# Inverse roots of four values per partition by a power on GpSimd

## The chip, the cores and the metric

The kernel runs on one core of a Trainium2 chip. The metric is the device time in microseconds from launch to the end of the program, the median of several executions. The engines are named as the profile names them: PE is TensorE (PEld its weight loads), DVE is VectorE, ACT is ScalarE, POOL is GpSimd and SP is SyncE, which issues most of the DMAs. Each engine works through its own queue in order, and waits on semaphores for the others.

## The reference

A residual stream x of four sequences of 512 rows and 128 features goes through twelve sublayers in four groups. Each group is half a feed-forward layer, a full attention layer, and the same feed-forward layer again, each on the normalized stream:

```python
def _layernorm(x, axis=-1, eps=1e-05):
    m = jnp.mean(x, axis=axis, keepdims=True)
    v = jnp.var(x, axis=axis, keepdims=True)
    return (x - m) / jnp.sqrt(v + eps)
...
    x = x + 0.5 * _L0_ffn_ref(_layernorm(x, axis=-1), ...)
    x = x + _L0_attn_ref(_layernorm(x, axis=-1), ...)
    x = x + 0.5 * _L0_ffn_ref(_layernorm(x, axis=-1), ...)
    x = x + 0.5 * _L1_ffn_ref(_layernorm(x, axis=-1), ...)
...
    x = x + 0.5 * _L3_ffn_ref(_layernorm(x, axis=-1), ...)
```

Group 0 has a feed-forward layer that selects neurons and a local attention with relative positions. Group 1's feed-forward layer is a transformer block with causal attention, two more layer norms (`var + LN_EPS` under an inverse root, LN_EPS 1e-5) and eight experts; its attention is linear, on queries and keys divided by their lengths. Group 2 has a feed-forward layer that sends each row to one of eight experts, and a block-local attention. Group 3's feed-forward layer is two transformer layers with windowed attention on unit-length queries and keys and a layer norm of its own; its attention is dense.

Inverse square roots stand in all the layer norms and in the unit lengths.

## The kernel before

The stream x stays in SBUF as 16 tiles of 128 rows by 128 features, four tiles to a sequence b, and y holds the normalized stream. A layer norm of a sequence is `statistics` (line 207): for each of its four tiles a BATCH_NORM_STATS and a BATCH_NORM_AGGREGATE on DVE, which give mean and variance in `ln_mv`, and then one `inverse_root` over the four variances of a partition, a 128x4 operand, into `ln_r`. Then `scaled` (line 220) writes the four tiles of y on DVE, one instruction each (L225), and `turn` (line 249) transposes them on PE (`pt_y`) and copies them on ACT to `yT` (L254), from which the sublayer's products read.

`inverse_root` (line 188) is an approximation: L195 adds or clips by a constant, L196 makes a first guess from the bits of the number, and two rounds refine it, each of three instructions on DVE (L198, L200, L201) or four on POOL (L198, L203, L204, L205). So it is eight small instructions on DVE or ten on POOL. All the calls, by width n:

- n = 4, on DVE: 52 calls of `statistics`. 48 are for the stream, four sequences at each of the twelve sublayers; four are group 1's own layer norms of the last sequence.
- n = 4, on POOL: 12 calls of `statistics` for group 1's own layer norms of the other three sequences (`l1_experts`, line 992). Their result goes to `scaled_by_act` (line 236), two small POOL instructions and four on ACT.
- n = 4 on POOL in 14 units of group 3's feed-forward layer (`variance`, line 1786), n = 4 on DVE in one unit, and n = 2 on DVE twice at the very end. There the variances come from a product with ones (`pvar`), DVE copies them to `rs` (L1793), and the result spreads over a diagonal `dg` on DVE (L1801, in `spread`) which a product (`pb`) carries to all partitions.
- n = 16 on POOL, 64 calls (`project`, line 1667), and n = 128 on DVE, four calls (`scale` of the linear attention, line 1142).

The order of the work has two sources. Products on PE, most of ACT and some of DVE are kept in the order of the program (`mm_in_order`, `keep_in_program_order`); which sequence's normalization runs beside which step is written into the program by chains of deferred parts (`chain`, `tick`, `leave_normed`). The remaining instructions of DVE and POOL are put in order at compile time by a planner which runs the program on its own estimates of durations; on the chip the queues are then worked in that fixed order.

POOL's other work matters where the change puts something into its queue:

- Group 1's causal attention: an affine select after each pair of exponentials (L835), which waits for ACT.
- Group 2's feed-forward layer ends with 16 indirect DMAs on POOL, one per tile (L1371), that gather the experts' rows into y. They are all issued in `l2_slots` ahead of the updates of x (L1379), which come sequence by sequence and are each followed by `leave_normed` with `statistics`.
- Group 3's feed-forward layer: sums and scalings of 128x1024 and 128x512 (L1668, L1669, L1731), and the n = 16 inverse roots.

Of the kernel before, what the change touches and what calls it, by code (L numbers as in the profile page):

```python
# [23 lines left out]
F32, I32 = mybir.dt.float32, mybir.dt.int32  # L24
AF = mybir.ActivationFunctionType
ALU = mybir.AluOpType
AX = mybir.AxisListType

P = 128
B, S, D, H, HD = 4, 512, 128, 16, 8  # L30
NT = B * S // P
TB = S // P
# [71 lines left out]
def tile_macaron(ctx, tc, x_in, const_in, vec_in, w0_in, ws_in, ws3_in, w2f_in, w3_in, out):  # L104
    nc = tc.nc
    pool = lambda name, **kw: tc.tile_pool(name=name, bufs=1, **kw)

    keep = ctx.enter_context(pool("keep"))
# [41 lines left out]
    make_identity(nc, ident)  # L150
    onesm = keep.tile([P, P], F32, name="onesm")
    nc.gpsimd.memset(onesm, 1.0 / D)
    ones = keep.tile([P, P], F32, name="ones")
    nc.gpsimd.memset(ones, 1.0)

# [32 lines left out]
    def inverse_root(sb, dst, src, name, op, c, eng=None):  # L188


        n = src.shape[-1]
        v = sb.tile([P, 3, n], F32, tag=name, name=name, bufs=2)
        eng = eng or nc.vector
        xx, yy, t = (v[:, i, :] for i in range(3))
        eng.tensor_scalar(xx, src, c, None, op)  # L195
        eng.tensor_scalar(yy.bitcast(I32), xx.bitcast(I32), -0.5, float(0x5F1FFFF9), ALU.mult, ALU.add)  # L196
        for to, a, b in ((yy, -0.703952253, 1.681913895), (dst, -0.50000016, 1.50000048)):
            eng.tensor_mul(t, yy, yy)  # L198
            if eng is nc.vector:
                eng.scalar_tensor_tensor(t, t, a, xx, ALU.mult, ALU.mult)  # L200
                eng.scalar_tensor_tensor(to, t, b, yy, ALU.add, ALU.mult)  # L201
            else:
                eng.tensor_mul(t, t, xx)  # L203
                eng.tensor_scalar(t, t, a, b, ALU.mult, ALU.add)  # L204
                eng.tensor_mul(to, t, yy)  # L205

    def statistics(src, b, eng=None, pinned=False):

        st = keep.tile([P, TB, 6], F32, tag="ln_st", name="ln_st", bufs=2)
        mv = keep.tile([P, TB, 2], F32, tag="ln_mv", name="ln_mv", bufs=3)  # L210
        r = keep.tile([P, TB], F32, tag="ln_r", name="ln_r", bufs=3)
        for t in range(TB):
            first = nc.vector.bn_stats(st[:, t, :], src[:, b * TB + t, :])
            if pinned and t == 0:
                tc.keep_in_program_order(first)
            nc.vector.bn_aggr(mv[:, t, :], st[:, t, :])
        inverse_root(keep, r, mv[:, :, 1], "ir4", ALU.add, 1e-5, eng)
        return mv, r
# [897 lines left out]
    def l1_attn(vms):  # L1116
        with pool("l1a") as sb, banks("l1aps", d=2, m=3, o=1):
# [19 lines left out]
            def scale(b):  # L1137

                qkv, vm = seqs[b]["qkv"], vms[b % 2]
                rn = sb.tile([P, TB * 32], F32, tag="rn", name="rn")  # L1140
                nc.vector.tensor_reduce(rn, seqs[b].pop("sq").rearrange("p t (h d) -> p (t h) d", d=HD), AX.X, ALU.add)
                inverse_root(sb, rn, rn, "ir128", ALU.max, 1e-24)
                beta = sb.tile([P, TB, H], F32, tag="beta", name="beta")
                nc.vector.tensor_add(beta, qkv[:, :, 384:400], rows(VEC(vec, "1a_bb"), TB))
                nc.scalar.activation(beta, beta, AF.Sigmoid)
                qk = qkv[:, :, 0:256].rearrange("p t (h d) -> p t h d", d=HD)
                r4 = rn.rearrange("p (t h) -> p t h", t=TB)[:, :, :, None].to_broadcast([P, TB, 32, HD])
                nc.vector.tensor_mul(qk, qk, r4)
                for t in range(TB):
                    a = vm[:, t, 0, 0:1]  # L1150
                    to = bass.AP(a.tensor, a.offset, [list(a.ap[0]), [32, 4], [D + HD, 4], [1, HD]])
                    nc.vector.tensor_mul(
                        to, qkv[:, t, 256:384].rearrange("p (g j d) -> p g j d", g=4, j=4),
                        beta[:, t, :].rearrange("p (g j) -> p g j", g=4)[:, :, :, None].to_broadcast([P, 4, 4, HD]),
                    )
# [437 lines left out]
    def l3_ffn(w3, tag, first, rb):  # L1593
        with pool(tag) as sb, banks(tag + "ps", d=3, m=2):
# [48 lines left out]
            def project(step):  # L1643
# [21 lines left out]
                rn = sb.tile([P, 16], F32, tag="rn", name="rn", bufs=6)  # L1665
                nc.vector.tensor_reduce(rn, sq, AX.X, ALU.add)
                inverse_root(sb, rn, rn, "ir16", ALU.max, 1e-24, nc.gpsimd)
                nc.gpsimd.tensor_add(t1, t1, t2)  # L1668
                nc.gpsimd.tensor_mul(t1[:, 8:16, :], t1[:, 8:16, :], bcast(rn[:, 8:16], 64))  # L1669
# [411 lines left out]
```

## Time and profile before

| | |
|---|---|
| median of three runs | 2732.9 us (2726.75 to 2735.28) |
| profiled execution | 2729.0 us |
| its span, first to last instruction | 2726.9 us |
| mean granted TensorE clock | 0.88 |
| PE busy | 2191.1 us (80%) |
| DVE busy | 1808.4 us (66%) |
| ACT busy | 1267.1 us (46%) |
| POOL busy | 905.4 us (33%) |

The program is a long row of stages with different limits, so a share of the whole span says little of one place. The views of the trace used below are the groups by tile (durations as least, median and largest, with who waited for them), the table of waits (engine and line, what it waited for, total us, times, longest), and the timeline (start, duration, engine, line, operation, what it writes and reads, and in brackets the idle time of the engine before it and what ended it).

### The profile page before, as it was taken

To read this page: it belongs to the slowest core of one execution; us is meant where nothing else is said; L and a number is where in the kernel's file an instruction comes from. 1 tells how busy PE (TensorE), PEld (TensorE's weight loads), DVE (VectorE), ACT (ScalarE), POOL (GpSimd) and SP (SyncE) were. 2 spreads that over 40 slices of the span, in tenths; PEclk is the share of its full clock that TensorE was granted. 3 is DMA by queue.
4 is the path that set the end of the run, shared out by engine and by line. 5 is a ranking of instruction groups with operands and counts; after the bars stand their busy time and mean duration, and the time that the engine had idled before them with its cause. 6 is when DMAs were issued, how large, how long until landed. Compare 5 with 4: busy or idle time off the path is not lost. (4 is left out here: it accounts for less than half of the span.)

```text
span 2726.9 us, 49905 instructions
## 1 busy us (share of the span) xinstructions
PE 2191.1 (80%) x18572; PEld 1226.1 (45%) x18572; DVE 1808.4 (66%) x5013; ACT 1267.1 (46%) x3067; POOL 905.4 (33%) x1678
## 2 busy tenths in 40 slices
PE   4277539988779999948666868898899999789888
PEld 2145214443334444438456745555433333455555
DVE  4746487777566777563664487777567775877774
ACT  3054314444333544314332356776525554667764
POOL 1012012233122222213321377766300000877761
PEclk8578769998789999868886889999879999899998
DMA  3053010000000000008104611000000000100000
GB/s 143 0 158 93 0 63 1 1 1 1 1 1 1 1 2 5 5 21 300 37 10 160 200 27 24 21 21 20 1 0 1 1 1 7 28 20 21 22 21 12
DMA packets 33930, 99.31 MB, mean 36 GB/s; under 512 B 6200, under 2 KB 12344, under 8 KB 33176
## 3 DMA queue, kind: packets, MB, share of 16 engines
q1 hardware_dynamic: 30760, 88.03, 10.0%
q0 software_dynamic: 2496, 5.12, 0.8%
q8 instruction: 146, 2.39, 0.4%
q10 hardware_dynamic: 432, 2.98, 0.3%
q14 instruction: 96, 0.79, 0.1%
HBM read 66.88 MB, written 14.55 MB: 30 GB/s over the span
## 5 line engine op out<-in xcount | busy, mean ns | idle before, releaser
L832 ACT ACTIVATE PT<-pk_at 128x512 f32<-128x512 f32 (+3 forms) x768 | 335.2, 488 | 405.4 <-PE pq_at L171 259.3
L171 PE MATMUL pk_at<-qx,km 32*128 32x512 f32 (+3 forms) x1536 | 398.8, 554 | 4.6 <-ACT PT L832 2.7
L804 DVE CUSTOM_DVE_ANT_0 s<-pq_at,cst 128x384 f32<-128x384 f32 (+3 forms) x512 | 249.9, 488 | 96.0 <-PE pq_at L171 42.5
L171 PE MATMUL pq_at<-km,qT 32*128 32x128 f32 (+3 forms) x1024 | 274.0, 500 | 16.0 <-DVE nm L804 12.0
L1607 ACT ACTIVATE s<-s,nm,rn 128x128 f32<-128x128 f32 x512 | 245.5, 482 | 0.9 <-DVE nm L1719 0.7
L835 POOL TENSOR_SCALAR_AFFINE_SELECT PT<-PT 128x256 f32<-128x256 f32 x256 | 104.5, 410 | 388.7 <-ACT PT L832 387.7
L171 PEld LDWEIGHTS pk_at<-qx,km 32*128 32x128 f32 x1536 | 146.7, 190 | 153.3 <-issue 92.9
L171 PE MATMUL po_at<-PT,vh 128*32 128x128 f32 (+3 forms) x2432 | 205.6, 394 | 8.5 <-POOL PT L835 8.4
L806 DVE TENSOR_REDUCE nm<-pq_at 128x1 f32<-128x512 f32 x256 | 165.6, 685 | 57.6 <-PE pq_at L171 57.2
L1668 POOL TENSOR_TENSOR t<-t,t 128x1024 f32<-128x1024 f32 x64 | 151.8, 2372 | 123.4 <-DVE t L1664 123.1
L171 PE MATMUL pq_at<-km,t 32*128 32x512 f32 x512 | 175.0, 670 | 1.6 <-DVE nm L806 1.2
L168 PE MATMUL pt_y<-ident,y 128*128 128x128 f32 x224 | 52.3, 362 | 132.2 <-DVE y L225 104.9
L171 PE MATMUL p_qk<-w,hT 128*128 128x512 f32 x256 | 141.9, 682 | 8.8 <-DVE t L1664 6.0
L254 ACT COPY yT<-pt_y 128x512 f32<-128x512 f32 x56 | 32.8, 585 | 239.1 <-PE pt_y L168 238.6
L168 PE MATMUL pt<-ident,s 128*128 128x128 f32 x640 | 93.0, 293 | 62.0 <-POOL s L1731 38.9
L1731 POOL TENSOR_TENSOR s<-s,sm 128x1024 f32<-128x1024 f32 x64 | 121.6, 1901 | 49.1 <-DVE sm L1730 41.0
L171 PEld LDWEIGHTS po_at<-PT,vh 128*32 128x32 f32 x2432 | 53.8, 109 | 173.3 <-issue 119.8
L171 PEld LDWEIGHTS pq_at<-km,qT 32*128 32x128 f32 x1024 | 110.2, 189 | 46.6 <-DVE nm L804 26.8
L1607 ACT ACTIVATE sq<-p_qk 128x1024 f32<-128x1024 f32 x64 | 65.6, 1026 | 118.4 <-PE p_qk L171 65.8
L168 PEld LDWEIGHTS pt<-ident,s 128*128 128x128 f32 x640 | 78.2, 150 | 93.7 <-POOL s L1731 48.1
L1661 DVE TENSOR_TENSOR t<-p_qk,w 128x1024 f32<-128x1024 f32 x64 | 78.2, 1223 | 55.7 <-ACT sq L1607 55.6
L1349 DVE SCALAR_TENSOR_TENSOR hT<-pa,w,sg 128x128 f32<-128x128 f32 x184 | 51.9, 345 | 85.4 <-ACT sg L1348 63.6
(435 smaller groups left out, 5167.6 us busy)
## 6 DMA issues: line engine op xcount, KB each, us to landing
w<-in_w2f_dram SPq DMA_DIRECT2D x46, 836.0 KB, 6.2
vb<-v SPq DMA_DIRECT2D x112, 128.0 KB, 2.2
skew<-qe SPq DMA_DIRECT2D x16, 512.0 KB, 3.0
rel<-skew SPq DMA_DIRECT2D x64, 128.0 KB, 3.5
w<-in_w_dram SPq DMA_DIRECT2D x1, 4147.0 KB, 12.5
w<-in_w_dram SPq DMA_DIRECT2D x1, 3200.0 KB
od<-o SPq DMA_DIRECT2D x46, 64.0 KB, 5.1
yd<-y SPq DMA_DIRECT2D x8, 256.0 KB, 2.3
```

Of the source, the lines that this page charges most:

```text
L168: return nc.tensor.transpose(dst, src, ident[: src.shape[0], : src.shape[0]])
L171: tc.keep_in_program_order(nc.tensor.matmul(dst, lhsT=lhsT, rhs=rhs, start=start, stop=stop))
L254: by_order(nc.scalar.copy(yT[:, b, :], pt))
L804: nc.vector.tensor_tensor_reduce(s[:, :nk], pq[:, :nk], causal[:, S - nk :], 1.0, -BIG, ALU.add, ALU.max, to)
L806: nc.vector.tensor_reduce(to, pq, AX.X, ALU.max)
L832: by_order(nc.scalar.activation(PT[:, i, q0:], pk[:, q0:], AF.Exp, scale=SC8))
L835: nc.gpsimd.affine_select(d, d, pattern=[[0, 2], [1, P]], base=0, channel_multiplier=-1, compare_op=ALU.is_ge, fill=0.0)
L1349: nc.vector.scalar_tensor_tensor(hT[s][:, c, :], pa[:, ts(c, P)], b1[:, c : c + 1], sg, ALU.add, ALU.mult)
L1607: tc.keep_in_program_order(nc.scalar.activation(*args, **kw))
L1661: nc.vector.tensor_mul(by_head(t1), by_head(p3), over(tab[:, 0]))
L1668: nc.gpsimd.tensor_add(t1, t1, t2)
L1731: nc.gpsimd.tensor_mul(s, s, bcast(sm, P))
```

## The change

Where n is at most 4, `inverse_root` now keeps its first instruction (add or clip) on the engine of the call, and POOL then raises the result to the power of a tile that holds -0.5, straight into the destination. The tile `minus_half`, 128x4, is set once at the start by a memset on POOL. The 16- and 128-wide calls are as before.

```diff
     onesm = keep.tile([P, P], F32, name="onesm")
     nc.gpsimd.memset(onesm, 1.0 / D)
+    minus_half = keep.tile([P, TB], F32, name="minus_half")
+    nc.gpsimd.memset(minus_half, -0.5)
...
         n = src.shape[-1]
+        if n <= TB:
+            v = sb.tile([P, n], F32, tag=name, name=name, bufs=2)
+            (eng or nc.vector).tensor_scalar(v, src, c, None, op)
+            nc.gpsimd.tensor_tensor(dst, v, minus_half[:, :n], ALU.pow)
+            return
         v = sb.tile([P, 3, n], F32, tag=name, name=name, bufs=2)
         eng = eng or nc.vector
```

## The prediction

> **What bounds the kernel now.** I read the page first: PE is busy 80% of the span and no engine is full, so stages and waits decide. The chain of waits can be followed only from 1812 us to the end; before that I go by the waits themselves. Then I asked for the tile `ir`, in which the inverse roots are made, for the table of waits, and for the timeline at three kinds of call.
>
> The tile `ir` (durations in ns, least/median/largest), then who waited for it:
>
> ```profile
> L198 POOL TENSOR_TENSOR ir<-ir x180: 198/215/218, 487.9 to 2682.6; 128x16 f32<-128x16 f32 x128, 128x4 f32<-128x4 f32 x52
> ...
> L198 DVE TENSOR_TENSOR ir<-ir x118: 127/161/2341, 11.7 to 2710.6; 128x4 f32<-128x4 f32 x106, 128x128 f32<-128x128 f32 x8, 128x2 f32<-128x2 f32 x4
> ...
> L205 POOL TENSOR_TENSOR rs<-ir x14: 198/199/202, 1666.2 to 2683.4; 128x4 f32<-128x4 f32 x14
> ...
>   DVE dg L1801: 47.1, 14
> ```
>
> A small two-input instruction on POOL takes 0.20 us, on DVE 0.16. DVE sits 47.1 us behind POOL's roots in group 3. The table of waits has the other end:
>
> ```profile
> POOL PT L835 <- ACT PT L832: 387.7, 215, 24.4
> ...
> PE pt_y L168 <- DVE y L225: 104.9, 21, 15.1
> ...
> POOL ln_m L240 <- DVE ln_r L201: 33.8, 2, 26.1
> ```
>
> 21 times PE stands still until a normalized tile comes: there the latency of the root counts in full. One such place, in the timeline:
>
> ```profile
> 1428.57 0.17 DVE L195 TENSOR_SCALAR ir<-ln_mv 128x4 f32<-128x4 f32 x1
> ...
> 1429.96 0.16 DVE L201 SCALAR_TENSOR_TENSOR ln_r<-ir 128x4 f32<-128x4 f32 x1
> 1430.16 1.12 DVE L225 TENSOR_SCALAR y<-x,ln_mv,ln_r 128x128 f32<-128x128 f32 x4
> ...
> 1430.65 1.15 PE L168 MATMUL pt_y<-ident,y 128*128 128x128 f32 x4 [2.61 <-DVE y L225]
> ```
>
> From the start of L195 to the start of L225 it is 1.59 us. The second kind, a unit of group 3:
>
> ```profile
> 2541.55 1.91 POOL L1731 TENSOR_TENSOR s<-s,sm 128x1024 f32<-128x1024 f32 x1
> ...
> 2543.54 0.23 POOL L195 TENSOR_SCALAR ir<-rs 128x4 f32<-128x4 f32 x1
> ...
> 2544.68 1.02 ACT L1607 ACTIVATE sq<-p_qk 128x1024 f32<-128x1024 f32 x1 [1.55 <-PE p_qk L171]
> ...
> 2546.11 0.20 POOL L205 TENSOR_TENSOR rs<-ir 128x4 f32<-128x4 f32 x1
> ...
> 2546.34 0.69 DVE L1801 SCALAR_TENSOR_TENSOR dg<-ident,rs 128x512 f32<-128x512 f32 x1 [3.32 <-POOL rs L205]
> ...
> 2546.95 1.22 DVE L1661 TENSOR_TENSOR t<-p_qk,w 128x1024 f32<-128x1024 f32 x1
> ```
>
> Ten POOL instructions take 2.77 us; L1661 could have started at 2545.71, when `sq` was done, and starts 1.3 us later. The third kind, after the gathers of group 2:
>
> ```profile
> 1307.58 0.94 POOL L1371 DMA_INDIRECT y<-od,at  x1 [20.22 <-DMA od<-o]
> ...
> 1326.34 0.94 POOL L1371 DMA_INDIRECT y<-od,at  x1 [0.31 <-issue]
> ...
> 1315.92 0.17 DVE L195 TENSOR_SCALAR ir<-ln_mv 128x4 f32<-128x4 f32 x1
> ...
> 1319.62 1.11 DVE L225 TENSOR_SCALAR y<-x,ln_mv,ln_r 128x128 f32<-128x128 f32 x4
> ...
> 1320.11 1.15 PE L168 MATMUL pt_y<-ident,y 128*128 128x128 f32 x4 [15.13 <-DVE y L225]
> ```
>
> Here the first sequence's root is made on DVE while POOL issues gathers one every 1.25 us, until 1327.28. The other feed-forward layer of group 2 ends the same way: gathers from 1544.00 to 1563.67, L225 at 1557.86, PE idle 8.81 until 1558.34.
>
> **The change part by part.** It removes seven DVE instructions at 55 calls (52 in `statistics`, three in group 3), 385 in all, some 71 us of DVE's busy time, and nine POOL instructions at 26 calls, 234 x 0.20 = 46 us. It adds 81 powers on POOL, a hop from DVE to POOL and back at 55 calls, and one memset of about 0.1 us at the start, which lies beside the first loads and costs nothing unless POOL holds the first call up.
>
> *The power, T.* No row shows one. It is no cheaper than the 128x4 product, 0.20. The far end is the ten-instruction root on POOL, 2.77, though nothing in the trace excludes more. The first end would mean that a power costs what a product does, so I build it up: 128x1024 takes 2.37 us (L1668) and 128x4 0.20, so one pass costs 2.1 ns a column. The exponent is a tensor, so the instruction must serve any exponent; I assume 100 to 150 elementary steps a column. That is 0.2 + 4 x (0.21 to 0.32) = 1.05 to 1.5. I take 1.3, and keep 0.2 and 2.77 for the range.
>
> [...]
>
> *The 55 calls on DVE.* After: L195 0.17, hop to POOL 0.14 (L1664 ends 2549.36, POOL's L1668 starts 2549.50), T, hop back 0.03 (2546.31 to 2546.34), so 0.34 + T against 1.59: even at T = 1.25. I count 23 places that are not hidden: 14 of the 21 PE waits (without the two at the gathers, one in group 3, and second tiles of the same sequence), the two `ln_m` waits, and seven in group 3 that the chain goes through. At T = 1.3: 23 x 0.05 = +1 us. The other calls lie beside PE work; their cover gone, each costs the same 0.05.
>
> *The 14 units of group 3.* The root on POOL goes from 2.77 to 0.28 + 1.3 = 1.58, 1.19 less. What is late next is `sq`: L1661 starts after it by 1.73, 1.32, 0, 0.16, 1.32, 0.89, 1.79, 0, 0.81, 1.32, 0, 0 us in the twelve full units, which caps the gain. With 1.19 as the limit that is 7.8, and 2 x 1.19 for the two last units of the layers, 10.2. POOL's sums and DVE's masks recur in the same loop, so I take 70%: -7.
>
> The 12 POOL calls of group 1 get 1.4 us shorter each. ACT's PE-bound exponentials cover them (6.3 us of waits on `ir` in all): 0.
>
> *The gathers.* All 16 stand in the program ahead of the updates, so I expect the first sequence's power behind the last of them. Its L225 then starts at 1327.31 + 1.3 + 0.03 instead of 1319.62, 9.0 late; in the second place at 1563.71 + 1.3 + 0.03 instead of 1557.86, 7.2 late. PE, which waits for exactly this, moves with it. Recovered: the second sequence's statistics, 2.9 us of DVE work after L225 now, can be done in the wait. +16.2 - 3 = +13. If the planner puts the power among the gathers, it is 0 (rival 3).
>
> *POOL's queue elsewhere.* Behind the power on POOL, and behind L225 on DVE, stand others: in group 1's attention affine selects that wait on average 1.8 us (387.7/215) for ACT, and on DVE the row maxima (L804), for whose banks PE waits. Five calls lie there: 5 x 1.8 = 9 if nothing covers it, 0 if the planner leaves room. PE works on the maxima five steps ahead (LEAD, line 718), so I take +4. Late in group 2 and in the first layers of group 3 DVE's small instructions are now held beside POOL's big ones (L198, 2341 ns at most against 161): seven fewer to be held, but L225 held in their place. 0, with 4 us either way.
>
> Sum: +1 - 7 + 13 + 4 = +11, so 2740 against the profiled execution's 2729.0 (its span 2726.9 and 2.1 around it). That execution stands 3.9 below the median of the three runs, 2732.9; on the median's footing it is 2744.
>
> **The rivals.** *1, faster: a short power.* At T = 0.5 the DVE calls give 23 x -0.75 = -17, the units -9 (all of the slack, 13.3 x 0.7), gathers +12, queues +3: -11, median 2722. It decides below T of about 0.6. For it: POOL's 16-wide rows cost hardly more than the 4-wide (215 against 198), so four columns may share their steps. Against it: no POOL row does more than one pass. Chance 0.25.
>
> *2, a long power.* At T = 1.8, columns one after the other: +13 - 4.5 + 14 + 5 = +27, median 2760. At 2.77: 23 x 1.52 = +35, units +3, gathers +16, queues +7 = +61, median 2794. At 5, each lane for itself: +86 +25 +21 +10 = +142, median 2875. Chance 0.28, of which 0.12 for near 1.8 and 0.08 for above 3.9.
>
> [...]
>
> *3, the gathers don't matter,* because the planner sets the power between them: T = 1.3 gives +1 - 7 + 4 = -2, no change, median 2731. For it: in the second place DVE takes the next sequence's update (L1379) between L195 and L196 of the first, so the planner thinks gathers quick. Chance 0.10.
>
> **How the numbers follow.** My forecast, T between 0.9 and 1.6 with the gathers in front, has 0.37, and 2744 is its time. Its own range is 2735 to 2753. For 8 in 10 I go down into rival 1 to T = 0.25 (23 x -1.0, -9, +11, 0 = -21, 2712) and up to T = 3.9 (some +100, 2835); about 0.1 stays out at each end. A measurement here can tell some 0.3%, 8.2 us. Faster by more (below 2724.7): three quarters of rival 1 and small parts of the forecast and rival 3, 0.25. Slower by more (above 2741.1): rival 2 and 0.6 of the forecast, 0.53 with a little of rival 3. Within: 0.22.
>
> **What would show it.** In the changed profile: a POOL row of 81 powers (128x4, two of 128x2) at about 1.3 us; the wait of `dg` on POOL's `rs` down from 3.3 to about 2.1 us each; L225 after the gathers at some 20 us after the first gather where it is 12 now, with PE's wait there up from 15.1 to 24; DVE some 70 us less busy. A power under 0.6 or over 1.8 makes the forecast wrong, and so does a power issued between two gathers, or another order on DVE that moves a whole stage.

## The result and the profile after

The changed kernel was first measured at 2720.1 us (median of seven executions, 2715.65 to 2726.1) beside 2735.28 for the kernel before (seven, 2726.75 to 2743.29): a ratio of 0.9951, 95% interval 0.9934 to 0.9967, so 13.4 us faster (18.1 to 9.0). The prediction was 2744, slower. Two later measurements of the same two kernels gave 1.0009 (0.9993 to 1.0025, no difference) and 0.9962 (0.995 to 0.9975, faster). So the question is also why one change has two results; the experiments answer most of it.

The profiled execution took 2719.6 us, its span 2716.7 (before: 2729.0 and 2726.9). The first part of the page after, busy time of each engine:

```profile
PE 2180.3 (80%) x18572; PEld 1222.5 (45%) x18572; DVE 1753.8 (65%) x4628; ACT 1267.3 (47%) x3067; POOL 943.6 (35%) x1526
```

DVE has 385 instructions fewer, as counted, and is 54.6 us less busy (1808.4 before), where the prediction had 71; POOL is 38.2 us more busy. The kernel has seven lines more above `statistics`, so the old L225 is now L232, L1801 is L1808, and the power is L197.

The groups of the tile `minus_half`, which every power reads (least/median/largest in ns), and who waited for them:

```profile
L197 POOL TENSOR_TENSOR ln_r<-ir,minus_half x64: 1002/1018/1546, 11.4 to 2307.1; 128x4 f32<-128x4 f32 x64
L197 POOL TENSOR_TENSOR rs<-ir,minus_half x17: 697/1037/1251, 1674.5 to 2700.2; 128x4 f32<-128x4 f32 x15, 128x2 f32<-128x2 f32 x2
...
  DVE y L232: 61.0, 43
  DVE dg L1808: 29.1, 16
```

Here are the 81 powers. T is 1.02 us at 128x4 and 0.70 at 128x2, so about 0.16 a column and 0.38 besides. DVE now waits 61.0 us for layer-norm roots, a wait that did not exist, and 29.1 us over 16 places for those of group 3 (47.1 over 14 before). The table of waits has the same from PE's side:

```profile
POOL ln_r L197 <- DVE ir L196: 388.5, 36, 107.3
POOL PT L842 <- ACT PT L839: 384.3, 218, 23.6
...
PE pt_y L170 <- DVE y L232: 74.3, 21, 12.9
...
PE pt_y L170 <- issue: 39.6, 2, 23.9
```

In the first row POOL stands at a power until DVE has done its first instruction; the 33.8 us that it waited at L240 for DVE's roots are gone into it. PE's two long waits behind the gathers (15.1 and 8.8 us before) are the 39.6 us of the last row, filed under "issue", for which the profile shows no releaser; without them 74.3 us are left where 104.9 less 23.9, so 81.0, stood before. The three kinds of call in the timeline, first the open place that stood at 1428.57:

```profile
1433.13 0.17 DVE L196 TENSOR_SCALAR ir<-ln_mv 128x4 f32<-128x4 f32 x1
1433.38 1.01 POOL L197 TENSOR_TENSOR ln_r<-ir,minus_half 128x4 f32<-128x4 f32 x1 [6.45 <-DVE ir L196]
1434.43 1.12 DVE L232 TENSOR_SCALAR y<-x,ln_mv,ln_r 128x128 f32<-128x128 f32 x4 [1.12 <-POOL ln_r L197]
```

From L196 to L232 it is 1.30 us, 1.59 before. A unit of group 3, with what comes behind its root:

```profile
2536.68 1.04 POOL L197 TENSOR_TENSOR rs<-ir,minus_half 128x4 f32<-128x4 f32 x1
...
2537.51 1.03 ACT L1614 ACTIVATE sq<-p_qk 128x1024 f32<-128x1024 f32 x1 [1.55 <-PE p_qk L173]
...
2537.75 0.69 DVE L1808 SCALAR_TENSOR_TENSOR dg<-ident,rs 128x512 f32<-128x512 f32 x1 [1.91 <-POOL rs L197]
...
2538.57 1.23 DVE L1668 TENSOR_TENSOR t<-p_qk,w 128x1024 f32<-128x1024 f32 x1
```

DVE waits 1.91 us for the root, 3.32 before, and L1668 now starts 0.03 after `sq` is done (2538.54): the slack is used up, as the prediction had it. And behind the first gathers:

```profile
1326.17 0.94 POOL L1378 DMA_INDIRECT y<-od,at  x1 [0.30 <-issue]
1327.14 2.05 POOL L197 TENSOR_TENSOR ln_r<-ir,minus_half 128x4 f32<-128x4 f32 x2
```
```profile
1328.72 1.15 PE L170 MATMUL pt_y<-ident,y 128*128 128x128 f32 x4 [23.86 <-issue]
```

The power stands behind the last gather, and PE waits 23.86 us for the tile where it waited 15.13; it starts 8.6 us later than before (1320.11). All of this is what the prediction described. Yet the total was the other way.

### The profile page after: what moved, and what is told of

It reads as the page before. It is cut to its first block, busy times and chain, and to the rows that moved or that the text cites. A ratio compares the mean times of both kernels' runs of the same rounds, so it can differ in the third digit from the quotient of the medians.

```text
span 2716.7 us, 49358 instructions
## 1 busy us (share of the span) xinstructions
PE 2180.3 (80%) x18572; PEld 1222.5 (45%) x18572; DVE 1753.8 (65%) x4628; ACT 1267.3 (47%) x3067; POOL 943.6 (35%) x1526
## 3 DMA queue, kind: packets, MB, share of 16 engines
q1 hardware_dynamic: 30760, 88.03, 10.2%
## 4 chain that ended last, share of the span: by engine, by line
PE 55%; DVE 23%; POOL 8%; ACT 8%; issue 5%; DMA 2%; POOLq 0%; DVEq 0%; SPq 0%; ACTq 0%
PE pk_at L173 10%; PE po_at L173 6%; PE pa L173 4%; PE pq_at L173 4%; PE pag L173 3%; PE po L173 3%; ACT s L1614 2%; PE pe L173 2%; PE p_qk L173 2%; DVE t L1671 2%; PE pg L173 2%; DVE t L1668 2%; PE pz L173 2%; POOL ln_r L197 2%; PE pt L170 2%
## 5 line engine op out<-in xcount | busy, mean ns | idle before, releaser
L842 POOL TENSOR_SCALAR_AFFINE_SELECT PT<-PT 128x256 f32<-128x256 f32 x256 | 104.8, 411 | 384.4 <-ACT PT L839 384.3
L197 POOL TENSOR_TENSOR ln_r<-ir,minus_half 128x4 f32<-128x4 f32 x64 | 65.9, 1032 | 389.8 <-DVE ir L196 388.5
L170 PE MATMUL pt_y<-ident,y 128*128 128x128 f32 x224 | 52.5, 360 | 138.5 <-DVE y L232 74.3
L173 PE MATMUL p_qk<-w,hT 128*128 128x512 f32 x256 | 136.6, 660 | 13.1 <-DVE t L1671 10.3
L1668 DVE TENSOR_TENSOR t<-p_qk,w 128x1024 f32<-128x1024 f32 x64 | 78.2, 1223 | 58.3 <-ACT sq L1614 57.5
```

The costliest lines, as they stand in the source:

```text
L170: return nc.tensor.transpose(dst, src, ident[: src.shape[0], : src.shape[0]])
L173: tc.keep_in_program_order(nc.tensor.matmul(dst, lhsT=lhsT, rhs=rhs, start=start, stop=stop))
L197: nc.gpsimd.tensor_tensor(dst, v, minus_half[:, :n], ALU.pow)
L842: nc.gpsimd.affine_select(d, d, pattern=[[0, 2], [1, P]], base=0, channel_multiplier=-1, compare_op=ALU.is_ge, fill=0.0)
L1668: nc.vector.tensor_mul(by_head(t1), by_head(p3), over(tab[:, 0]))
```

## The experiments

Names: the units are the roots of group 3 (14 on POOL; the runs that change them change the three short roots of DVE with them), "the gathers' calls" the eight `statistics` behind the two sets of gathers, "POOL's calls" the 12 of group 1. Differences in us are the ratio less one, times the median of the kernel before in the same measurement, with the 95% interval in brackets. Two traces are lined up by PE's instructions, which come in the same order in both: the difference of their starts shows where one kernel gains or loses.

### First measurement: parts of the change, and twice its length

**Steps behind the gathers.** The eight calls keep the approximation steps, all others have the power:

```diff
-        if n <= TB:
+        if n <= TB and not steps:
...
-            leave_normed(b, spare, gap, True)
+            leave_normed(b, spare, gap, True, steps=True)
```

> The power everywhere but in the eight calls right after the two sets of gathers, which go back to the eight steps on DVE. Theory A (each place counts for itself): the changed kernel starts the stage after the gathers 8.6 and 6.9 us late, and of the first 4.8 is caught up later, so this one is some 11 us faster than the changed kernel, 21 to 27 below the kernel before; PE's first product after the gathers comes about 12.5 us after the first gather again. Rival B (the delay is absorbed by what follows, or replaced by another wait): within 4 us of the changed kernel, 10 to 16 below the kernel before.

Measured 0.9972 (0.9956 to 0.9989): 7.6 us below [12.0, 3.0]. Neither case: taking the delay away gained nothing over the changed kernel.

**The units alone.** The power only in `spread`'s roots:

```diff
-        if n <= TB:
+        if power:
...
-                inverse_root(rb, rs[:, :n], rs[:, :n], f"ir{n}", ALU.add, 1e-5, eng)
+                inverse_root(rb, rs[:, :n], rs[:, :n], f"ir{n}", ALU.add, 1e-5, eng, True)
```

> The power in group 3's own layer norm alone (17 calls: 14 units on POOL, one on DVE, two halves at the end), the old steps everywhere else. Theory A: the units give 12 us (the sum of the changes of PE's time from unit to unit in the changed profile) and the ends of the two layers 2 to 6: 13 to 18 us below the kernel before. The forecast's own term was 7. Rival B (group 3's gain in the changed profile comes from another order of DVE and POOL or from the clock, not from the shorter root): under 5.

Measured 0.998 (0.9957 to 1.0002): 5.5 below [11.7 below, 0.5 above], with executions from 2715.7 to 2734.9. Not settled by this run.

**DVE's 52 calls alone,** the gathers' among them:

```diff
+        inverse_root(keep, r, mv[:, :, 1], ..., ALU.add, 1e-5, eng, eng is None or eng is nc.vector)
```

> The power in the 52 calls of the layer norms on DVE alone, POOL's calls and group 3's units as before. Theory A: the gathers cost 11 net, some 21 other open places give 0.2 us each and what DVE is spared gives a little more: 0 to 8 us above the kernel before. Rival B (these calls gain more than the gathers cost, by the shorter DVE queue): 3 or more below it.

Measured 1.0018 (1.0003 to 1.0032): 4.9 above [0.8, 8.7]. It fits the first case, but the trace gave a reason to doubt the reading, below.

**Twice the power.** A power with exponent 1 ahead of each:

```diff
-            nc.gpsimd.tensor_tensor(dst, v, minus_half[:, :n], ALU.pow)
+            nc.gpsimd.tensor_tensor(v2, v, ones[:, :n], ALU.pow)
+            nc.gpsimd.tensor_tensor(dst, v2, minus_half[:, :n], ALU.pow)
```

> Every root is made by two powers, one with exponent 1 and then the one with -0.5, so each is 1.0 to 1.1 us longer, all else as in the changed kernel. Theory A with all the open places of the forecast (23 calls on DVE, 14 units, two gathers): 30 to 40 us above the changed kernel, 15 to 28 above the kernel before. Rival B (most places have slack): less than 12 above the changed kernel, still not slower than the kernel before.

Measured 1.0196 (1.0161 to 1.0232): 53.5 above before [44.0, 63.4]. The first of the two powers took 1.04 us at the median (1001 to 1546 ns) and the second 1.01, so an exponent of 1 costs what -0.5 costs. That is more than either case allowed. Against the changed kernel, some 10 below before where it was measured under the same conditions (fourth measurement), it is some 64 us for about 1.04 more in 81 places, as if some 60 of the 81 were open at that length. A part may be the clock: its mean was 0.8728 against 0.8817 for before beside it, and among the 25 executions of before 0.001 of clock goes with 1.8 us, which would make some 16 of the 64. The prediction had counted 23 open calls, 14 units and the gathers. Cover that is enough for a root of 1.6 us seems not to be enough for one of 2.3.

**What the traces showed.** In the first two of these kernels nothing behind the gathers was changed, and still PE stood 4 to 7 us later there than in the trace of before. DVE's instructions of 0.16 us came one every 1.40 us in the second place (1563.43, 1564.84, 1566.23, 1567.63, 1569.03 in the first kernel), each released late by the one ahead of it. In the trace of before they follow each other by 0.20. The kernels with the tile `minus_half` have all later tiles further on in SBUF (by 32 bytes of a partition, as the next expectation reckons; no view shows it), y among them, into which the gathers write; so the next measurement tried the place of y.

### Second measurement: the place of y

**The tile alone,** no power:

```diff
     nc.gpsimd.memset(onesm, 1.0 / D)
+    minus_half = keep.tile([P, TB], F32, name="minus_half")
+    nc.gpsimd.memset(minus_half, -0.5)
```

> The kernel before with the tile minus_half and its memset and nothing else: no power anywhere. The tile takes 32 bytes of a partition, so y and all tiles behind it begin 32 bytes later. In the traces of the two kernels that keep the approximation steps after the gathers, DVE's instructions there are released only every 1.40 us (1563.43, 1564.84, 1566.23, 1567.63, 1569.03, each 0.16 long), and PE gets its next product 4.1 us late after the first set of gathers and 6.3 us late after the second. Theory P (the place of y does it): the same stalls here, both places together some 10 us, so 6 to 12 us above the kernel before, without any change of the roots. Theory C (chance of one profiled execution, or something that the powers do): no such spacing here, and the time within 3 us of before.

Measured 1.0016 (1.0 to 1.0032): 4.4 above [0.0, 8.7]. Theory P falls: the trace has no late releases behind the gathers. The median alone would not have told it, for the identical program later came out 3.0 above itself.

**Steps behind the gathers, with a tile of 64 bytes:**

```diff
-    minus_half = keep.tile([P, TB], F32, name="minus_half")
+    minus_half = keep.tile([P, 16], F32, name="minus_half")
```

> As in the run that keeps the approximation steps in the eight calls after the gathers and uses the power everywhere else, but minus_half is 128x16, 64 bytes of a partition, so y lies 64 bytes later than before instead of 32. Theory P: the stalls behind the gathers go away, some 10 us, so 15 to 21 us below before, where that run was 7.2 below; it is then 3 to 8 us below the changed kernel of the same job. Theory C: as that run, 4 to 11 below before, not below the changed kernel. Either way no call in it waits behind the gathers, so if it comes out level with the changed kernel, the 8.6 and 7.0 us by which PE starts later behind the gathers there are not what the total shows.

Measured 2711.09, 0.9968 (0.9956 to 0.9981): 8.7 below [12.0, 5.2]. That is theory C's size, but the kernel is 13.7 below the changed kernel of the same measurement (2724.82, next), which C excluded. No late releases in the trace.

**The changed kernel again:**

> The changed kernel itself, for a second trace and for a comparison within this job. Both theories: ratio to before near 0.995, 10 to 18 us below. In the trace L232 behind the gathers is about 20.8 us after the first gather again, and the stretch of the half clock near 681 to 698 us of the kernel before may or may not come back: if it does, its 7 us were never the roots'.

Measured 2724.82 beside 2720.22, 1.0009 (0.9993 to 1.0025): 2.4 above [1.9 below, 6.8 above]. Not the first result: the kernel before is 15 us faster than beside the first result (2735.28), the changed one is 5 slower (2720.1).

**The changed kernel with the tile of 64 bytes:**

> The changed kernel with minus_half 128x16, so that y lies as it does in the run with the steps kept and the wide tile. Behind the gathers DVE has nothing to do here but to wait for the power, so slow releases cost little. Theory P: within 4 us of the changed kernel, a little faster if anything (PE's first eight products there took 6.78 us instead of 5.94). Theory C: the same within 3 us.

Measured 2725.14, 1.0018 (1.0004 to 1.0031). The width of the tile does nothing (2724.82 with 16 bytes). And against the kernel that differs only in the gathers' calls, 2711.09, these calls cost 14.0 us here.

So in this measurement nobody's releases were late, whatever the place of y, and in the one before all four kernels had them late or were waiting for the power at that time. That leaves the kernel before itself as the one that changes.

### Third measurement: the kernel before again, and two parts

**The kernel before:**

> The kernel before itself, for a second trace of it. Theory S (on some chips DVE's releases are slow while the gathers write, whatever the kernel; the first four experiments ran on one such chip and the next four did not): either the trace has the releases spaced by 1.2 to 1.4 us in the second set of gathers and PE's 4.1 us wait in the first, and then the median is near 2731; or it has neither, and then it is near 2720. Theory L (the kernels with the power cause it): never slow here, and the median may lie anywhere from 2720 to 2733. The half clock at 681 to 698 us: no forecast; if it is absent the stretch 668 to 712 takes about 37 us instead of 44.

Measured 2723.34 beside 2720.55, 1.0011 (0.9997 to 1.0024): the same program differs from itself by 3.0 [0.8 below, 6.5 above], which is what these comparisons are good for. The releases are prompt.

**The power in the gathers' calls alone,** against the kernel with the steps there:

```diff
-        if n <= TB and not steps:
+        if n <= TB and steps:
```

> The power only in the eight calls behind the two sets of gathers, everything else as before (minus_half 128x16). The first trace gave PE a start 8.6 and 7.0 us later there, with 4.8 made up in the first place. Theory G (that delay stays in the total): 10 to 16 above before if the releases there are prompt in the kernel before; with slow releases, which cost before some 10 us that this kernel hides behind its own wait, 0 to 6 above. Theory H (made up later): within 4 of before on a chip with prompt releases.

Measured 1.0064 (1.0047 to 1.0082): 17.4 above [12.8, 22.3]. Theory G, a little above its range: the delay stays in the total. PE's first wait there is 23.87 us. Lined up with the second trace of before, PE loses 8.8 us at the first gathers, wins 4.5 back and loses 7.0 at the second, 11 in all; the two kernels that differ in these calls alone (2711.09 and 2725.14) are 13.5 apart there. So not all of the 17.4 is seen at the gathers.

**The units alone,** tile of 64 bytes:

> The power only in group 3's 14 units, minus_half 128x16. The root there goes from 2.77 us to some 1.3 us (0.23 for the first instruction, 1.02 for the power), 1.5 less, capped by the slack before sq (10.3 us in the rows of twelve units) and two tails of 1.5. Theory U (the slack sets the gain): 8 to 14 below before. Rival (POOL's sums and DVE's masks take it back): 0 to 6 below.

Measured 0.9955 (0.9939 to 0.997): 12.2 below [16.6, 8.2]. Theory U: the slack sets the gain.

**The 16-wide roots as one power too,** on the kernel with the steps behind the gathers:

```diff
-        if n <= TB and not steps:
+        if n <= 16 and not steps:
```

> The 64 roots of sixteen values on POOL as one power as well, on top of the kernel that keeps the steps behind the gathers (minus_half 128x16). Rows: 128x4 in 1.02 us, 128x2 in 0.70, so 0.16 a column and 0.38 fixed, and 128x16 would take 2.9; the ten instructions from the start of L195 to the end of L205 take 3.0 (1570.78 to 1573.76). Theory W (cost grows by the column): rows of 2.8 to 3.0 us plus 0.3 for the first instruction, time within 4 us of 2711's place, that is 5 to 13 below before. Rival V (columns share their steps beyond some width): rows of 1.2 to 2 us, and 4 to 12 us faster than that.

Measured 0.997 (0.9958 to 0.9982): 8.2 below [11.4, 4.9]; that kernel without it was 8.7 below. Theory W. Its row, by the tile `minus_half`:

```profile
L197 POOL TENSOR_TENSOR rn<-ir,minus_half x64: 2928/2929/3147, 1570.7 to 2633.2; 128x16 f32<-128x16 f32 x64
```

2.93 us for 16 columns: 0.70, 1.02 and 2.93 lie on one line, 0.16 a column. Columns share nothing but the 0.38. The ten instructions take 3.0 us for 16 columns and 2.77 for four, so the gain is gone at 16.

### Fourth measurement: both kernels where releases are late

**The kernel before, and the changed kernel:**

> The kernel before once more, for what it does on a chip with slow releases. If the job's chip is one: the releases behind the gathers spaced by 1.2 to 1.4 us, PE some 4 and 6 us later there than in the two traces of it so far, and a median near 2731. If not: near 2720 to 2723, and the releases prompt.

> The changed kernel on the same chip. With slow releases in the kernel before: 10 to 16 below it. With prompt ones: 0 to 7 above it, as in the second measurement (2.4 above, interval 1.9 below to 6.8 above).

Before: 2731.82 beside 2732.32, 0.9999 (0.9985 to 1.0013). Changed: 0.9962 (0.995 to 0.9975), 10.4 below [13.7, 6.8]. This time the kernel before has the late releases itself. Its third trace, DVE behind the second gathers:

```profile
1563.39 0.16 DVE L196 TENSOR_SCALAR ir<-ir 128x4 int32<-128x4 int32 x1
1564.95 0.16 DVE L198 TENSOR_TENSOR ir<-ir 128x4 f32<-128x4 f32 x1 [1.40 <-issue]
1567.05 0.17 DVE L200 SCALAR_TENSOR_TENSOR ir<-ir 128x4 f32<-128x4 f32 x1 [1.94 <-remote]
1567.79 0.16 DVE L201 SCALAR_TENSOR_TENSOR ir<-ir 128x4 f32<-128x4 f32 x1 [0.57 <-DVE ir L200]
1569.18 0.16 DVE L198 TENSOR_TENSOR ir<-ir 128x4 f32<-128x4 f32 x1 [1.23 <-DVE ir L201]
```

and its second trace, the same instructions of the same program:

```profile
1551.00 0.16 DVE L196 TENSOR_SCALAR ir<-ir 128x4 int32<-128x4 int32 x1
1551.19 0.16 DVE L198 TENSOR_TENSOR ir<-ir 128x4 f32<-128x4 f32 x1
1551.39 0.16 DVE L200 SCALAR_TENSOR_TENSOR ir<-ir 128x4 f32<-128x4 f32 x1
1551.59 0.16 DVE L201 SCALAR_TENSOR_TENSOR ir<-ir 128x4 f32<-128x4 f32 x1
1551.78 0.16 DVE L198 TENSOR_TENSOR ir<-ir 128x4 f32<-128x4 f32 x1
```

Behind the first gathers it is PE that stands, in the third trace, with a releaser that the profile cannot name:

```profile
1322.70 3.78 PE L171 MATMUL p<-yT,ws 128*128 128x512 f32 x4 [0.73 <-issue]
1330.51 3.78 PE L171 MATMUL p<-yT,ws 128*128 128x512 f32 x4 [4.02 <-remote]
```

where the second trace has the eight products in one go:

```profile
1314.69 5.88 PE L171 MATMUL p<-yT,ws 128*128 128x512 f32 x8 [0.73 <-ACT yT L254]
```

Lined up, the third trace falls behind the second by some 5 us at the first gathers and some 6.5 at the second, 11 to 12 in all. The medians beside them differ by as much (2732.3 and 2720.6), but the two spans by 25.3: the third trace loses another 6.6 near 690, where its clock stood at 0.50, and the rest in small pieces. And the mean clock of before was lower too in this measurement, 0.8810 against 0.8838 in the third, so that the medians alone could not tell the releases from the clock; the rows above do. The changed kernel has DVE and PE waiting for the power during just these microseconds. Its trace here, lined up with that of the second measurement, loses nothing at either set of gathers (0.0 us). It pays its 8.6 and 7.0 us there in either case, and nothing on top.

**POOL's calls alone:**

```diff
+        inverse_root(keep, r, mv[:, :, 1], ..., ALU.add, 1e-5, eng, eng is not None and eng is not nc.vector)
```

> The power only in the 12 calls of group 1 that are made on POOL, everything else as before (minus_half 128x16). Each gets about 1.5 us shorter. Theory N (ACT's exponentials cover them, as the prediction had it): within 3 us of before. Rival (POOL's queue reaches the affine selects earlier): 3 to 8 below.

Measured 0.9964 (0.9952 to 0.9976): 9.8 below [13.1, 6.6], more than the rival said. In the second trace of before POOL works two of these roots at once, and what is behind them are the affine selects (L835):

```profile
1090.42 0.41 POOL L195 TENSOR_SCALAR ir<-ln_mv 128x4 f32<-128x4 f32 x2 [1.05 <-DVE ln_mv L216]
...
1094.70 0.41 POOL L241 TENSOR_SCALAR ln_m<-ln_m 128x4 f32<-128x4 f32 x2
1095.07 0.41 POOL L835 TENSOR_SCALAR_AFFINE_SELECT PT<-PT 128x256 f32<-128x256 f32 x1
```
```profile
1098.66 3.18 ACT L244 ACTIVATE y<-y,ln_m,ln_r 128x128 f32<-128x128 f32 x8
```

With the power (here L842 is the select, L251 the scaling):

```profile
1086.74 0.41 POOL L196 TENSOR_SCALAR ir<-ln_mv 128x4 f32<-128x4 f32 x2 [1.05 <-DVE ln_mv L223]
1087.12 2.02 POOL L197 TENSOR_TENSOR ln_r<-ir,minus_half 128x4 f32<-128x4 f32 x2
...
1089.93 0.77 POOL L842 TENSOR_SCALAR_AFFINE_SELECT PT<-PT 128x256 f32<-128x256 f32 x2
```
```profile
1092.54 3.18 ACT L251 ACTIVATE y<-y,ln_m,ln_r 128x128 f32<-128x128 f32 x8
```

The select comes 3.19 us after the root's start instead of 4.65, ACT's scaling 5.80 instead of 8.24. PE's instructions lined up, the third trace of before against this one, move forward by 0.5 to 2.5 us at six of these places (0.5 at 580, 1.5 at 650, 1.6 at 720, 1.1 at 950, 2.5 at 1100, 0.9 at 1170). Near 970 they fall 2.7 back, where this trace has the clock at 0.50 (962.4 to 969.2) and that one has not.

**DVE's 44 calls away from the gathers:**

```diff
+        inverse_root(keep, r, mv[:, :, 1], ..., ALU.add, 1e-5, eng, (eng is None or eng is nc.vector) and not steps)
```

> The power in the 44 calls on DVE that don't stand behind the gathers, everything else as before (minus_half 128x16). From the start of the first instruction to the start of the scaling such a call went from 1.59 to 1.30 us in the trace of the changed kernel. Theory D (the 23 open places gain 0.29 each): 4 to 9 below before. Rival Q (the powers in POOL's queue, and another order on DVE, cost as much): 2 below to 6 above. The difference of the two kernels measured so far (the units alone 12.2 below; units, POOL's calls and these 44 together 8.7 below) speaks for Q.

Measured 1.0022 (1.0011 to 1.0033): 6.0 above [3.0, 9.0]. Rival Q: the calls got shorter and the kernel slower. The traces show where: PE's instructions that stand at 540 to 1240 us in the second trace of before, nearly all of group 1, take 699.8 us there, 706.8 in the third trace and 712.5 here. Elsewhere this kernel is no slower than the third trace. PE is busy 591.6 us of that stretch, against 582.8 and 587.7, at the same instructions and a lower granted clock, so a good part of the loss is longer products and not waiting alone (columns: window, length, busy time of PE, PEld, DVE, ACT and POOL, granted clock, DMA share, GB/s; second trace, third trace, this kernel):

```profile
540.18:1240.02 699.84, 582.82 (x4330) 290.20 (x4323) 470.25 (x1805) 265.21 (x647) 183.11 (x401) 0.89 0.03 10
542.08:1248.91 706.83, 587.72 (x4329) 292.38 (x4322) 470.25 (x1805) 265.13 (x647) 183.00 (x401) 0.88 0.03 10
539.76:1252.24 712.48, 591.63 (x4330) 293.66 (x4322) 455.88 (x1693) 265.10 (x647) 199.66 (x417) 0.87 0.03 10
```

### The version that the parts point to

The power where a root of ten instructions stood on POOL, and in the three short roots of group 3's ends; DVE's layer norms keep their steps:

```diff
+        inverse_root(keep, r, mv[:, :, 1], ..., ALU.add, 1e-5, eng, eng is not None and eng is not nc.vector)
...
+                inverse_root(rb, rs[:, :n], rs[:, :n], f"ir{n}", ALU.add, 1e-5, eng, True)
```

> The power where a ten-instruction root stood on POOL (the 12 calls of group 1 and the 14 units of group 3) and in the three short roots of group 3's ends; all 52 calls of the layer norms on DVE keep their steps (minus_half 128x16). Alone the units gave 12.2 below before and group 1's calls 9.8 below. Theory A (they add): 16 to 24 below before, the fastest of all. Rival K (the granted clock takes a part back, as in the kernel that has the power everywhere but behind the gathers, whose mean clock was 0.0026 lower and which came to 8.7 below where its parts add to 16): 7 to 14 below, with a mean clock lower than that of before.

Measured 2716.82 beside 2736.16, 0.9923 (0.9905 to 0.9942): 21.1 below [26.0, 15.9]. Theory A: they add (22.0 by the parts). The mean granted clock of its executions was 0.8812, that of before beside it 0.8785; rival K asked for a lower one. A clock that is 0.0026 higher would go with some 4 to 6 of the 21.1 us, at the 1.5 to 2.1 us per 0.001 of the larger sets of executions; whether the shorter roots raised it is not shown.

## Why the prediction was wrong

Each term of the sum, and what the run of that part alone measured:

| Term | predicted, us | measured alone, us |
|---|---|---|
| T, 128x4 | 1.3 | 1.02 |
| gathers' calls | +13 | +17.4 [12.8, 22.3]; 14.0 between two kernels that differ in nothing else |
| units of group 3 | -7 | -12.2 [-16.6, -8.2] |
| POOL's calls of group 1 | 0 | -9.8 [-13.1, -6.6] |
| DVE's other calls, and POOL's queue | +1 and +4 | +6.0 [3.0, 9.0] |
| sum | +11 | +1.4 |
| the changed kernel, releases prompt | | +2.4 [-1.9, 6.8] |
| the changed kernel, releases late | | -13.4 [-18.1, -9.0] and -10.4 [-13.7, -6.8] |

Two steps of the sum were mis-sized most: POOL's calls of group 1, put at 0, gained 9.8 us, and the units gained 12.2 instead of 7; with the parts as measured the sum is +1.4 instead of +11, so no change where a slower kernel was forecast. And the footing failed, which made the first result faster.

*The footing.* The sum was made against a trace in which DVE's instructions behind the gathers are released promptly, and set on a median, 2732.9, that lies with the medians of late releases (2730.7, 2732.3 and 2736.2; where they were prompt 2720.2 and 2720.6). That the profiled execution took 2729.0 all the same has another cause in part: from 681.3 to 698.4 us its TensorE clock stood at 0.50, and lined up with the second trace, where it stood at 1.00, it loses 6.7 us there, of the 11.4 between the two spans. No trace of before with late releases was kept from the first result. But the traces bear a mark: those with prompt releases have 6198 to 6200 landings of DMAs recorded, all others 5782 to 5868, and the first trace of the changed kernel has 5860, the first trace of before 6200. So the first pair of traces stems from the two conditions. The step of the gathers was right in its place and size, and the kernel before pays 11 to 12 us of the same cost where releases are late. Of these the changed kernel pays nothing, as it waits for the power then: +1.4 becomes some -10, beside -10.4 and -13.4 measured. No row of the first trace could have shown this, since it is not in it.

*T* was 0.28 shorter than taken, inside the bounds that the forecast set (0.9 to 1.6), so rivals 1 and 2 are both out. That it came so near has some luck in it: no row showed the 100 to 150 steps a column. At 2.1 ns a step the measured 0.16 us would be some 76, and the fixed part was 0.38 where 0.2 was taken. Nor does any run show the 1.8 of rival 2: over the same 0.2 it is 0.4 us a column, more than twice the measured 0.16. The first power of the kernel, at 11.45 us, took 1.03, as the later ones did (1.02 at the median).

*DVE's calls.* The hop was right, 0.28 + T against the 0.34 + T taken. With T = 1.02 the 23 places would gain 23 x 0.29 = 6.7 us; instead the 44 calls cost 6.0. What fails here is the step from the length of the root to its effect. Shown is that it doesn't carry over, and that the loss lies in group 1; two things were found that go with it, and how much belongs to which stays open. The powers stand in POOL's queue in group 1, as the term +4 had it. And the mean granted clock of the executions was lower, 0.8776 against 0.8810 for before beside them. Among the 23 executions of the kernel before there, 0.001 of clock goes with 1.5 us, so this difference would go with some 5 us. How the clock takes time back is seen at the start of group 1's attention, in the second measurement's changed kernel against the second trace of before; the same 32 products, the second time at a clock of 0.50 (747.80 to 751.20):

```profile
747.62 1.08 PE L171 MATMUL po_1a<-PT,vm 128*32 128x128 f32 x32
```
```profile
747.98 1.94 PE L173 MATMUL po_1a<-PT,vm 128*32 128x128 f32 x32
```

From the products `pb` to the fourth `pe` behind them it takes 23.2 us in the one (739.06 to 762.23) and 27.0 in the other (738.17 to 765.16), at clocks of 0.93 and 0.76, by the table of windows (columns as above):

```profile
738.00:764.00 26.00, 20.84 (x149) 10.72 (x142) 14.65 (x40) 5.41 (x12) 4.18 (x5) 0.93 0.00 1
```
```profile
737.00:767.00 30.00, 24.85 (x137) 12.68 (x130) 14.10 (x40) 5.00 (x11) 4.10 (x5) 0.76 0.00 1
```

*The units* gained 12.2 where -7 was taken. The working ahead of the 70% gave 10.2 at T = 1.3. At T = 1.02 the root is 1.47 shorter; capped at that, the slack of the rows gives 8.8 (9.3 uncapped, not the 10.3 that the expectation names), and two tails of 1.47 make it 11.7. (Read from the rows, a slack is some 0.08 smaller than listed, 1.24 and not 1.3 in the unit shown; it changes the sum by less than 1.) So the 70% for POOL's sums and DVE's masks was the mistake: the middle of the measurement has nothing taken back, though its interval just reaches 70% of 11.7.

*POOL's calls of group 1* were set to 0 on the ground that ACT's exponentials cover them, read from the 6.3 us of waits on `ir`. Those waits are what stands behind the root at once. The affine selects behind it on POOL, and the scaling in ACT's order behind the exponentials (which wait for PE's `pq_at` and `pk_at`, 259.3 and 134.2 us in the first trace of before), were late with it and filed under other names. Only the queue shows that, not the table of waits.

*Rival 3* (a power between two gathers) did not happen; the power stands behind the last one. The *held instructions* were taken as 0; no run separated them.

*What does not add up:* the units, POOL's calls and the 44 calls sum to -16.0, and the kernel with exactly these was 8.7 below [12.0, 5.2]. Its clock was 0.8807 against 0.8833 beside it, which would go with some 4 to 6 of the 7 missing us, while the units and POOL's calls alone had a clock 0.0012 and 0.0015 above that of before beside them. That the clock is the reason was not shown.

## What to carry to other kernels

Before a sum is set on a median, take a second trace of the kernel before: a trace shows one execution, and this kernel had 11 to 12 us behind the gathers that one trace had and another had not. Replace a chain by one instruction first where the chain already stands on that instruction's engine: 26 such roots, and three short ones of DVE with them, gave 21.1 us, while moving 52 chains to the other engine cost 17.4 behind the gathers and 6.0 elsewhere. When a chain gets shorter, read what is queued behind it on its own engine, not only who waits for its result.

## What was not expected of the hardware

**Late releases.** In three of the five measurements with experiments, DVE's releases during and up to 3 us after the two sets of indirect DMAs came up to 1.9 us late each (1.2 to 1.4 mostly), in all six kernels whose steps stand there (behind the first set PE's second four products wait 4.10, 4.13, 4.02 and 3.95 us in four of them); in the other two, none. It is not the program (both in the kernel before), not the place of y (the same tile ahead of it with prompt releases and with late ones), and not a lasting property of a chip (one chip, by its number, was prompt in the second measurement and late in the last). The records of those stretches also lack some semaphore updates: 11168 of the engines' updates are recorded in the third trace of before and 11230 in the second, and 5799 landings of DMAs against 6200. Every execution here has a recorded span and clock, so no run tells whether the recording itself has a part in it. What decides it is open.

**A power's price.** 0.38 us and 0.16 a column of 128 partitions, by the 0.70, 1.02 and 2.93 us of 2, 4 and 16 columns; with an exponent of 1 it took 0.70 at two columns and 1.04 at four.

**The clock.** The granted clock stood at 0.50 from 681.3 to 698.4 us in the first trace of before, while PE was busy for 17.07 of 17.10 us; in the second trace it is 1.00 from 674 to 701. The third trace has it again at the same instructions (682.3 to 699.3, PE busy 16.98 of 17.00; the mean from 672 to 712 is 0.79), so one program runs with it and without. A busy PE goes with either clock here: it was busy for 3.26 of the 3.40 us ahead of that stretch, at 1.00, and for 17.07 of 17.10 in it, at 0.50. What halves the clock and what ends it is not shown.
